# A two-layer GraphSAGE block with residual and layer norm: the stages of a node block moved and spaced otherwise, h2 produced turned, half-bank strips, degrees as rows

## The chip, the cores and the metric

The kernel runs on one core of one Trainium2 chip. The time is that of the device, in microseconds (us), as the median of several runs. Each profile is one execution of its own, recorded by the hardware profiler; its time and its span, from the first to the last instruction, are given beside the median.

The core's engines are named as in the profile: PE is TensorE's matmul, PEld its weight load, DVE VectorE, ACT ScalarE, POOL GpSimd, and SP SyncE, which here only starts DMA transfers.

## The reference, cut to what matters

12,500 nodes with 256 features each, 200,000 directed edges, sorted by their destination. `src` is uniform; `dst` is 12500 times the square of a uniform number, so low node numbers have many edges and high ones few. All is float32.

```python
def _sage_conv(x, src, dst, W_l, b_l, W_r):
    msgs = x[src]
    agg = jax.ops.segment_sum(msgs, dst, num_segments=N_NODES)
    deg = jax.ops.segment_sum(jnp.ones((src.shape[0],), x.dtype), dst, num_segments=N_NODES)
    mean = agg / jnp.maximum(deg, 1.0)[:, None]
    return mean @ W_l + b_l + x @ W_r

h = jax.nn.relu(_sage_conv(x, src, dst, W1_l, b1, W1_r))
h = jax.nn.relu(_sage_conv(h, src, dst, W2_l, b2, W2_r))
out = _layernorm(x + (h @ W3 + b3), axis=-1)        # eps 1e-5, no scale, no shift
```

All six weights and products are 256 by 256. The output has 12,500 rows of 256.

## The kernel before, in words

*Units.* The nodes are cut into NB = 98 blocks of 128 (P). D is 256 and NC = 2 is the number of 128-wide chunks in it. Two tables of layer results stand in device memory: `h_d` (h in float32) and `h3_d` (each float32 number as three bfloat16 parts, which `exact` makes). `x3_d` is the same split of x; the profile calls these two tables `x_d` and `h_d` in places.

*Two ways to sum neighbours.* The sums of the first nodes, which have many edges, are made by dense products: `count` builds a matrix that tells how often each source occurs for each of DN = 256 destinations, and `product` multiplies the split table with it. This covers HG1 = 5 groups of 256 nodes in layer 1 and HG = 8 in layer 2. The other nodes are summed from gathered rows.

- `count`: DVE builds one-hot pieces (`pick`, `low`, `aft`, L738, L741, L746), PE multiplies them (L765, L776, L780), ACT casts the product into `counts` (L782).
- `product`: SP loads `rows` of the table (L693), two blocks of 128 at a time, and PE multiplies them with the counts into `dense_ps` (L707); in layer 2 a second group goes `beside`, its counts streamed back from memory (L697). ACT copies the result into `d_sb` (L716).
- `degrees`: after each product of layer 1, 98 one-column products for each of the group's two blocks of 128 nodes (L797), with the counts as the stationary matrix and a column of ones as the moving one; DVE takes max(deg, 1) and its reciprocal into a column of `rdeg`.
- `Gathers`: 504 rounds over both layers. `gathered` issues four indirect DMAs on GpSimd's queue (L262), and PE multiplies the rows that landed with a selection matrix `one` into four strips of 32 destinations in `part_ps` (L274). After the last round of a group of edges ACT copies the strips into `some` (L284). `summed` multiplies `some` with a second selection `two` (L290, and L296 for the degrees in layer 1) and DVE adds the result to a ring: the degree row `degs` (L300) and the sums `sums` (L304). The ring is addressed by a register, so every reader of the ring waits for the latest adder.

*A block.* Each block of 128 nodes goes through a generator, whose `yield`s cut it into stages. `first_block`, three stages: load x rows, store the ring's degree row to `deg_d` | read it back as a column, transpose the x rows on PE (L902, copied from PSUM by ACT at L904 into `own_t`) | `sage`: two products with W_l (L925) and two with W_r (L930), zeroing of the ring's part by ACT (L933), two DVE steps with the bias and 1/deg (L936, L937), relu on ACT (L939), then the stores of h and its split. `last_block`, five stages: load the h rows | transpose them (L902) | `sage` | transpose h2 (L902, with `own_t` from L904) | product with W3 (L997), residual, layer norm (L999 to L1008), store (L1010). `agg` is `d_sb` for nodes with dense products and the ring for the others.

*What sets the order.* `layer` (L602) writes the order out by hand. Each round has three places (`part` 0, 1, 2). A place runs, in this order: in part 2, `summed` for the strips that the round before ended; then `pieces`, which moves one block on by one stage and begins another if fewer than MOST = 2 are under way; then `fill`, which takes dense and counting work from a generator until a budget of estimated costs (`COST_DENSE`, `COST_DEGREES` and others, `D_1`, `D_2`) is spent. A stage of a block comes no sooner than APART = 2 places after its last one:

```python
for part in range(3):
    if part == 2 and before:
        gathers.summed(*before, done)
        ...
    pieces()
    fill(spent + (due - spent) / (3 - part))
```

PE and GpSimd execute in the written order. The order on DVE, ACT and SP is the scheduler's, by its own estimates. PSUM is allocated by pools: `mixed_pool` with two banks for the sums and the transposed rows (and, in layer 1, the blocks' products), `part_pool` with one bank for the strips, `dense_pool`, `block_pool`, `beside_pool`, and `count_pool` with two buffers in layer 1 and one in layer 2.

*Tails.* A layer ends when its queue of blocks is empty. `left` keeps the dense work clear of the last 8 rounds of layer 1 and the last 14 of layer 2. A second path, `by_sorting`, is taken for other distributions of edges; it does not run here, and the diff does not touch it.

## Time and profile before

| | |
|---|---|
| runs | 3265.1, 3281.22 and 3290.72 us; median 3281.22 |
| profiled execution | 3281.46 us; span 3279.7 us; mean granted TensorE clock 0.888 |
| busy in the span | PE 2574.5 us, POOL 1967.7, PEld 1733.1, DVE 1566.5, ACT 1151.6 |
| PE, dense products with rows (L707) | busy 981.6 and 570.3 us; idle before them 58.9 and 24.2 |
| PE, counts (L776, L765) | idle before them 145.0 and 77.4 us |
| PE, first products of blocks (L925) | six groups; idle before them 69.7, 85.0, 1.5, 8.6, 5.8 and, for L930, 0.1 us |
| PE, transposes (L902) of x, h2, h | idle before them 6.8, 51.4 and 6.4 us |
| PE, degrees (L797) | busy 40.2 us, idle before them 25.1 |
| DMA | 612.56 MB, mean 187 GB/s |

The span less PE's busy time leaves 705 us in which PE does nothing. A line of a group gives the line number, the engine, the operation, its output and inputs by the program's names, the shape, the number of instructions, then after the first bar the busy time and the mean ns of one, and after the second the idle time of the engine just ahead of these instructions and what ended most of it. In the view of waits a line gives the engine, the output and line that waited, the instruction that ended the wait, and then the sum in us, the number of waits and the longest. In a timeline the columns are the start and the length in us, the engine, the line and the instruction, and in brackets a wait ahead of it with what ended it.

### The profile page before, as it was taken

To read this page: it belongs to the slowest core of one execution; us is meant where nothing else is said; L and a number is where in the kernel's file an instruction comes from. 1 tells how busy PE (TensorE), PEld (TensorE's weight loads), DVE (VectorE), ACT (ScalarE), POOL (GpSimd) and SP (SyncE) were. 2 spreads that over 40 slices of the span, in tenths; PEclk is the share of its full clock that TensorE was granted. 3 is DMA by queue.
4 is the path that set the end of the run, shared out by engine and by line. 5 is a ranking of instruction groups with operands and counts; after the bars stand their busy time and mean duration, and the time that the engine had idled before them with its cause. 6 is when DMAs were issued, how large, how long until landed. Compare 5 with 4: busy or idle time off the path is not lost.

```text
span 3279.7 us, 56146 instructions
## 1 busy us (share of the span) xinstructions
PE 2574.5 (79%) x18946; PEld 1733.1 (53%) x18946; DVE 1566.5 (48%) x5560; ACT 1151.6 (35%) x2331; POOL 1967.7 (60%) x2026
## 2 busy tenths in 40 slices
PE   4565668878878878889865887878889888888876
PEld 2122335545546656656643555556556666666654
DVE  6778675544445555555552122334345444343334
ACT  0423664444444444455441001223233333221122
POOL 6665666666665656666664666565666666556652
PEclk9766679979979989989987899989989999999998
DMA  5565668658658758647644566565556656566642
GB/s 123 164 185 171 179 205 274 209 159 262 209 156 289 225 174 266 221 144 238 222 142 122 181 183 184 176 181 166 177 167 192 184 170 183 164 200 198 204 139 84
DMA packets 375242, 612.56 MB, mean 187 GB/s; under 512 B 72111, under 2 KB 253989, under 8 KB 374949
## 3 DMA queue, kind: packets, MB, share of 16 engines
q1 hardware_dynamic: 273235, 343.33, 34.0%
q0 software_dynamic: 96768, 264.37, 26.7%
q8 instruction: 155, 2.54, 0.3%
q10 hardware_dynamic: 4946, 1.19, 0.2%
q14 instruction: 138, 1.13, 0.1%
HBM read 518.75 MB, written 89.92 MB: 186 GB/s over the span
## 4 chain that ended last, share of the span: by engine, by line
PE 59%; issue 8%; another core or an unknown queue 7%; DVE 5%; ACT 3%; DMA 3%; POOL 0%; ACTq 0%; DVEq 0%; SPq 0%; POOLq 0%
PE dense_ps L707 16%; PE part_ps L274 7%; PE count_ps L776 7%; PE beside_ps L707 6%; PE block_ps L925 6%; PE block_ps L930 5%; PE sum_ps L290 4%; PE block_ps L997 3%; PE block_ps L902 3%; DMA rows<-x_d 2%; ACT counts L782 2%; PE count_ps L780 1%; PE sum_ps L296 1%; PE dense_ps L797 1%
## 5 line engine op out<-in xcount | busy, mean ns | idle before, releaser
L262 POOL DMA_INDIRECT got<-in_x_dram,src_t x1076 | 1067.8, 992 | 649.6 <-issue 258.2
L262 POOL DMA_INDIRECT got<-h_d,src_t x940 | 897.7, 955 | 617.1 <-issue 230.8
L707 PE MATMUL dense_ps<-counts,rows 128*128 128x256 bf16 x5292 | 981.6, 282 | 58.9 <-issue 31.5
L707 PEld LDWEIGHTS <-rows 128*128 128x128 bf16 x7644 | 745.2, 101 | 327.6 <-issue 165.6
L782 ACT CAST counts<-count_ps 128x882 f32 (+3 forms) x688 | 611.3, 888 | 533.1 <-PE count_ps L776 135.6
L707 PE MATMUL beside_ps<-spare,rows 128*128 128x256 bf16 x2352 | 570.3, 282 | 24.2 <-issue 23.2
L776 PE MATMUL count_ps<-pick,low 128*128 128x490 bf16 (+2 forms) x1188 | 378.7, 371 | 145.0 <-ACT counts L782 64.3
L274 PE MATMUL part_ps<-got,one 128*32 128x257 f32 (+1 forms) x4032 | 385.4, 434 | 53.2 <-issue 21.7
L738 DVE TENSOR_SCALAR pick<-steps,key_t 128x686 bf16<-128x686 f16 (+3 forms) x816 | 332.6, 410 | 117.6 <-remote 32.1
L218 DVE TENSOR_TENSOR one<-lo_t,lane_b 128x128 f32<-128x128 bf16 x504 | 144.1, 286 | 470.7 <-remote 150.1
L284 ACT COPY some<-part_ps 128x257 f32<-128x257 f32 (+1 forms) x355 | 132.8, 374 | 643.4 <-remote 293.7
L741 DVE TENSOR_SCALAR low<-lanes,low_t 128x130 bf16<-128x130 f16 x816 | 221.0, 272 | 212.4 <-remote 72.5
L304 DVE TENSOR_TENSOR sums<-sums,sum_ps 128x256 f32 x355 | 145.6, 410 | 250.2 <-remote 110.6
L290 PE MATMUL sum_ps<-two,some 128*128 128x128 f32 x1420 | 241.1, 296 | 13.1 <-issue 8.3
L290 PEld LDWEIGHTS sum_ps<-two,some 128*128 128x128 f32 x1420 | 211.2, 207 | 32.2 <-issue 19.3
L776 PEld LDWEIGHTS <-low 128*128 128x128 bf16 x1188 | 121.1, 103 | 181.9 <-issue 62.7
L936 DVE TENSOR_TENSOR own<-block_ps,biases 128x256 f32<-128x256 f32 x196 | 82.4, 420 | 220.3 <-PE block_ps L930 106.5
L274 PEld LDWEIGHTS part_ps<-got,one 128*32 128x32 f32 x4032 | 89.1, 113 | 184.1 <-issue 161.1
L925 PE MATMUL block_ps<-w1l_sb,sums 128*128 128x256 f32 x352 | 123.5, 483 | 69.7 <-issue 31.5
L933 ACT COPY sums<-zero 128x256 f32<-128x256 f32 x170 | 68.7, 404 | 306.0 <-PE block_ps L930 142.6
L904 ACT COPY own_t<-block_ps 128x256 f32<-128x256 f32 x294 | 109.3, 375 | 183.4 <-remote 65.4
L746 DVE TENSOR_SCALAR aft<-steps,after_t 128x98 bf16<-128x98 f16 x689 | 173.6, 252 | 0.0
(184 smaller groups left out, 2678.7 us busy)
## 6 DMA issues: line engine op xcount, KB each, us to landing
rows<-x_d SPq DMA_DIRECT2D x245, 384.0 KB
rows<-h_d SPq DMA_DIRECT2D x196, 384.0 KB
count_d<-counts SPq DMA_DIRECT2D x28, 896.0 KB
spare<-count_d SPq DMA_DIRECT2D x196, 128.0 KB
x_sb<-in_x_dram SPq DMA_DIRECT2D x194, 128.0 KB
x_d<-split SPq DMA_DIRECT2D x98, 192.0 KB
h_d<-split SPq DMA_DIRECT2D x98, 192.0 KB
got<-in_x_dram,src_t POOLq DMA_INDIRECT x1076
```

What stands on the lines that cost most here:

```text
L262: rows = nc.gpsimd.indirect_dma_start(out=g[:, j, :D], out_offset=None, in_=self.table, in_offset=bass.IndirectOffsetOnAxis(ap=src_t[:, e: ...
L274: strip = nc.tensor.matmul(part_ps[j * W:(j + 1) * W, :width], lhsT=one[:, j], rhs=g[:, j, :width], start=r == 0, stop=r == n - 1)
L290: nc.tensor.matmul(sum_ps[:, c], lhsT=some[:, c * P:(c + 1) * P], rhs=two, start=True, stop=True)
L304: nc.vector.tensor_add(own, own, sum_ps[:, :NC])
L707: nc.tensor.matmul(t[:, c], lhsT=rows[:, b % 2, k, c * P:(c + 1) * P], rhs=d, start=False, stop=b == NB - 1 and k == 2 and c == NC - 1)
L738: nc.vector.tensor_scalar(r[:, :w * NB], steps[:, :w * NB], key_t[g][:, t - lo_g:t - lo_g + 1], None, op0=OP.is_equal)
L741: nc.vector.tensor_scalar(low.rearrange("p (a b) -> p a b", a=5), lanes_5[:, :, :LW // 5], low_t[:, t:t + 1], None, op0=OP.is_equal)
L746: nc.vector.tensor_scalar(aft.rearrange("p (a b) -> p a b", a=7), steps_7[:, :, :NB // 7], after_t[g][:, t - after_from[g]:t - after_from[ ...
L776: nc.tensor.matmul(c[:, a * NB:b * NB], lhsT=s, rhs=r[:, a * NB:b * NB], start=True, stop=alone)
L782: nc.scalar.copy(to[:, :, bass.ds(off_act.at(t), w)], c.rearrange("p (d s) -> p s d", s=NB))
L925: product = nc.tensor.matmul(ps[:, 0], lhsT=agg[:, c], rhs=wl[:, c], start=c == 0, stop=c == NC - 1)
L930: product = nc.tensor.matmul(ps[:, 1], lhsT=own_t[:, c], rhs=wr[:, c], start=c == 0, stop=c == NC - 1)
```

## The change

Four things are changed; the numbers of the lines in this section are those of the kernel before.

1. *Order and distance.* `pieces` stands ahead of `summed` in a place. Each stage yields the number of places to the next one: SOON = 2 from a block's loads to its transposes, APART = 4 after that.
2. *h2 turned.* In `last_block` the weights become the stationary matrices and the turned sums and rows the moving ones, so that the products come out with the features of h2 on the partitions. There are eight products of 128 columns in the place of four of 256. 1/deg is now needed along the free axis: the degree row is read from `deg_d` broadcast to 128 partitions (`r_sb`). The bias of layer 2 is a column for each partition (`b2_t`), added by ACT with the relu, in two halves. The transposes of h2 and their copy are gone, and with them one stage of five. `sage` is dissolved into the two blocks.
3. *Strips.* `part_ps` is one bank allocated once; layer 2's groups of rounds use its halves in turn.
4. *Degrees as rows.* In `degrees` the ones are the stationary matrix and the counts the moving one: 490 products with one output row of 256 columns in the place of 980 with one output column. Max and reciprocal are taken on the row, which is stored to `deg_d`. For blocks of the ring, max and reciprocal are taken on the ring's row before it is stored. Every block now reads its degrees back from `deg_d`, and `rdeg` is gone. `D_1`, layer 1's estimated cost of a dense group, falls accordingly.

```diff
+    part_bank = part_pool.tile([P, 2 * D], F32, name="part_ps")
@@ gathered
-            if r == 0:
-                self.part_ps = part_pool.tile([P, D + 1], F32, name="part_ps")
-            part_ps, width = self.part_ps, self.width
+            width = self.width
+            half = gr % 2 * D if self.second else 0
+            part_ps = part_bank[:, half:half + width]
@@ layer
-    MOST, APART = 2, 2
+    MOST, SOON, APART = 2, 2, 4
...
-                next(p)
-                queue.append([b, p, n_pieces - 1, turn + APART])
+                queue.append([b, p, n_pieces - 1, turn + next(p)])
...
-                next(q[1])
-                q[2:] = q[2] - 1, turn + APART
+                q[2:] = q[2] - 1, turn + next(q[1])
...
             for part in range(3):
+                pieces()
                 if part == 2 and before:
                     gathers.summed(*before, done)
                     ...
-                pieces()
                 fill(spent + (due - spent) / (3 - part))
@@ degrees
-        for j in range(DN // P):
-            for b in range(NB):
-                nc.tensor.matmul(ps[:, 0, j:j + 1], lhsT=c_sb[:, b, j * P:(j + 1) * P], rhs=ones_b,
-                                 start=b == 0, stop=b == NB - 1)
-                if b % 14 == 13:
-                    yield COST_DEGREES
-        deg = work.tile([P, DN // P], F32, name="d_deg", bufs=1)
-        nc.vector.tensor_scalar(deg, ps[:, 0, :DN // P], 1.0, None, op0=OP.max)
-        nc.vector.reciprocal(rdeg[:, n0:n0 + DN // P], deg)
+        for b in range(NB):
+            nc.tensor.matmul(ps[0:1, 0], lhsT=ones_b, rhs=c_sb[:, b, :DN], start=b == 0, stop=b == NB - 1)
+            if b % 14 == 13:
+                yield COST_DEGREES
+        deg = work.tile([1, DN], F32, name="d_deg", tag="own")
+        nc.vector.tensor_scalar(deg, ps[0:1, 0], 1.0, None, op0=OP.max)
+        nc.vector.reciprocal(deg, deg)
+        nc.sync.dma_start(deg_d[n0:n0 + DN // P].rearrange("b p -> (b p)")[None, :], deg)
-    D_1 = NB * COST_DENSE + DN // P * (NB // 14) * COST_DEGREES
+    D_1 = NB * COST_DENSE + NB // 14 * COST_DEGREES
@@ first_block
             agg, deg_row = ring(b)
+            nc.vector.tensor_scalar(deg_row, deg_row, 1.0, None, op0=OP.max)
+            nc.vector.reciprocal(deg_row, deg_row)
             nc.sync.dma_start(deg_d[b:b + 1], deg_row)
-        yield True
+        yield SOON
-        if of_ring:
-            deg = work.tile([P, 1], F32, name="deg")
-            with nc.allow_non_contiguous_dma(reason="a row becomes a column"):
-                nc.sync.dma_start(deg, deg_d[b, :, None])
+        deg = work.tile([P, 1], F32, name="deg")
+        with nc.allow_non_contiguous_dma(reason="a row becomes a column"):
+            nc.sync.dma_start(deg, deg_d[b, :, None])
         x_t, copied = transposed(x_sb, turned(), "own_t")
-        yield True
-        if of_ring:
-            nc.vector.tensor_scalar(deg, deg, 1.0, None, op0=OP.max)
-            nc.vector.reciprocal(rdeg[:, b:b + 1], deg)
-        h, own = sage(x_t, copied, b, agg, of_ring, w1l_sb, w1r_sb, biases[:, 0], "h")
+        yield APART
+        # the products, DVE steps and relu of sage, written out, with deg for rdeg[:, b:b + 1]
+        ...
@@ last_block
-        h2, _ = sage(h_t, copied, b, agg, of_ring, w2l_sb, w2r_sb, biases[:, 1], "h")
+        r_sb = work.tile([P, P], F32, name="r_sb")                # ahead of the transposes
+        nc.sync.dma_start(r_sb, deg_d[b:b + 1].to_broadcast([P, P]))
...
+        ps = block_bank()
+        for side, (t, w) in enumerate(((agg, w2l_sb), (h_t, w2r_sb))):
+            for o in range(NC):
+                for c in range(NC):
+                    product = nc.tensor.matmul(ps[:, side, o * P:(o + 1) * P], lhsT=w[:, c, o * P:(o + 1) * P],
+                                               rhs=t[:, c], start=c == 0, stop=c == NC - 1)
+                    ...
+        if of_ring:
+            zeroed(agg, product)
+        own = work.tile([P, NC, P], F32, name="own")
+        nc.vector.tensor_tensor(own, ps[:, 0].rearrange("p (c l) -> p c l", c=NC),
+                                r_sb.unsqueeze(1).to_broadcast([P, NC, P]), op=OP.mult)
+        nc.vector.tensor_add(own, own, ps[:, 1].rearrange("p (c l) -> p c l", c=NC))
+        h2_t = work.tile([P, NC, P], F32, name="h")
+        for c in range(NC):
+            nc.scalar.activation(h2_t[:, c], own[:, c], AF.Relu, bias=b2_t[:, c:c + 1])
         x_sb = load_rows(x, N, b, "x_sb")
-        yield True
-        h2_t, _ = transposed(h2, turned(), "own_t")
-        nc.vector.tensor_add(x_sb, x_sb, biases[:, 2])
-        yield True
+        yield APART
+        nc.vector.tensor_add(x_sb, x_sb, biases[:, 1])
         y = block_bank()
...
-    layer(Gathers(h_d, True), last_block, 5, staged(stages_2), cost_of(stages_2), 14)
+    layer(Gathers(h_d, True), last_block, 4, staged(stages_2), cost_of(stages_2), 14)
```

More of the change, by code (lines that the diff above doesn't have):

```diff
@@ L283, in gathered @@
             some = chosen_pool.tile([P, D + 1], F32, name="some", bufs=2)
-            nc.scalar.copy(some[:, :width], part_ps[:, :width])
+            nc.scalar.copy(some[:, :width], part_ps)
             return gr, some, two
@@ L919, in overlap, with zeroed @@
                 nc.scalar.copy(degs[:, RN:], zeros[0:1, 0])
[L921 to L940 removed]
+    def zeroed(agg, product):
+        cleared = nc.scalar.copy(agg, zeros)
+        tc.add_manual_dep(cleared.ins, product.ins.name, LANDED, reason="it signals for all")
     def block_bank(turned=False):
@@ L982, in last_block @@
         of_ring = agg is None
-        yield True
+        yield SOON
         if of_ring:
```

55 lines of the change are left out of this document (27 added, 28 removed).

## The prediction

> **What bounds the kernel now.** I read the page's busy times first, then the tensor engine's waits, then its groups with shapes kept apart, and last the timeline for the pace of each kind of product.
>
> ```profile
> PE 2574.5 (79%) x18946; PEld 1733.1 (53%) x18946; DVE 1566.5 (48%) x5560; ACT 1151.6 (35%) x2331; POOL 1967.7 (60%) x2026
> ```
>
> ```profile
> PE count_ps L776 <- ACT counts L782: 64.3, 52, 9.9
> PE block_ps L925 <- issue: 46.7, 26, 4.5
> ...
> PE block_ps L925 <- DVE sums L304: 36.4, 24, 6.4
> ...
> PE block_ps L902 <- ACT h L939: 34.6, 29, 3.7
> ...
> PE block_ps L925 <- ACT own_t L904: 29.4, 12, 5.8
> PE dense_ps L707 <- DMA rows<-x_d: 26.3, 19, 5.7
> ```
>
> The tensor engine is busy 2574.5 of 3279.7 us, nothing else comes near. GpSimd is not the limit: four gathers of 1.25 us make 5.0 us a round, rounds come every 6.1 to 6.5 us, and in the view of all waits GpSimd stands 332.7 us waiting for strips (L274). So the 705 us in which PE is idle are the price list. The lines of blocks (L925, L902, L997) hold 247 us of them by the groups, and these are what the change works on.
>
> ```profile
> L902 PE MATMUL block_ps<-ident,h 128*128 128x128 f32 x196 | 42.8, 302 | 51.4 <-ACT h L939 34.6 <-issue 14.4 <-ACT own_t L904 1.2
> L797 PE MATMUL dense_ps<-ones_b,counts 128*128 128x1 bf16 x980 | 40.2, 165 | 25.1 <-issue 18.2 <-ACT d_sb L716 6.4 <-DMA h_d<-split 0.5
> ```
>
> The mean of one record (302 ns) is its latency; the pace is the distance of two starts:
>
> ```profile
> 661.46 0.49 PE L797 MATMUL dense_ps<-ones_b,counts 128*128 128x1 bf16 x14 [2.03 <-ACT d_sb L716]
> 661.81 0.37 PE L776 MATMUL count_ps<-pick,low 128*128 128x490 bf16 x1
> ```
>
> ```profile
> 3061.19 0.27 PE L707 MATMUL beside_ps<-spare,rows 128*128 128x256 bf16 x1
> 3061.30 0.61 PE L290 MATMUL sum_ps<-two,some 128*128 128x128 f32 x4
> 3061.75 0.38 PE L902 MATMUL block_ps<-ident,h 128*128 128x128 f32 x2
> 3061.96 0.27 PE L707 MATMUL dense_ps<-counts,rows 128*128 128x256 bf16 x1
> ```
>
> So 14 one-column products take 0.35 us (25 ns each), 256 bfloat16 columns 0.11, four records of 128 float32 columns 0.45 (an instruction in float32 leaves two records), and the two transposes of a block 0.21.
>
> The last view shows a first product that waits for the sums:
>
> ```profile
> 1302.27 0.22 PE L296 MATMUL sum_ps<-two,some 128*1 128x128 bf16 x1
> ...
> 1302.94 0.64 PE L274 MATMUL part_ps<-got,one 128*32 128x257 f32 x8
> 1305.05 0.27 DVE L300 TENSOR_TENSOR spare<-spare,sum_ps 1x128 f32 x1 [1.73 <-PE part_ps L274]
> 1305.26 0.40 DVE L304 TENSOR_TENSOR sums<-sums,sum_ps 128x256 f32 x1
> 1305.81 0.45 PE L925 MATMUL block_ps<-w1l_sb,sums 128*128 128x256 f32 x1 [2.22 <-issue]
> ```
>
> L925 reads the ring, so it waits for the latest L304, here until 3.5 us after the sum's products; "issue" hides that cause. To price this, I took for each of the 196 blocks the PE work that stands in program order between the last sum and its first product (columns at the pace above), beside the idle time ahead of that L925 in the timeline (layer 2 without its tail after 3100 us):
>
> | work since the last sum, us | layer 1: blocks, mean idle | layer 2 |
> |---|---|---|
> | under 0.8 | 11, 1.58 | 7, 1.32 |
> | 0.8 to 1.1 | 18, 1.98 | 1, 6.38 |
> | 1.1 to 1.5 | 8, 1.35 | 11, 1.01 |
> | 1.5 to 2 | 11, 0.38 | 0 |
> | 2 to 3 | 22, 0.08 | 22, 0.15 |
> | 3 to 5 | 17, 0.08 | 26, 1.47 |
> | over 5 | 11, 0 | 13, 0.23 |
>
> A product within 1.5 us of a sum waits; later ones do not, except 3 to 5 us in layer 2, where nine wait for the copy of the turned rows (ACT own_t, up to 5.8 us) at two places' distance.
>
> **The change, part by part**, against the profiled execution: 3281.5 us, of which 3279.7 are its span; it stands at the median, 3281.2.
>
> *The transposes of h2 go.* 98 pairs of 0.21 us are 21 us, 23 at the granted clock of 0.888; with them the 51.4 us of idle. The wait for ACT's relu moves to the product with W3 four places later, over 8 us of other work where 2 to 3 us stood. I take 47 of the 51 as gone (some "issue" will show elsewhere): -70, between -75 and -50 (half of the idle returns). ACT loses a copy (0.375) and a relu of 256 columns (0.416) and gets two of 128, between the 0.295 of L1005 and 0.416: nothing on PE's path while ACT is 35% busy.
>
> *h2 from stationary weights.* Eight products of 128 columns for four of 256: sixteen records at the pace of L290 take 1.80 us; L925 and L930 take 0.94 and 0.87. So 0, up to +15. The page "TensorE: Matmul & The Clock Gate" of the Trainium skill (Back-to-back issue gap) says that the spacing of matmuls with a fresh weight load each is set by both, about 81 ns at 128 columns where the columns alone take 56; L290, a fresh load for each product, shows none of that here. By that ratio of the Trainium skill the sixteen records would take some 2.6 us, an estimate, and the 98 blocks +78 us.
>
> *Degree rows.* 980 one-column products (24.5 us at full clock, 27.6 at 0.888, and 25.1 idle: 52.7) become 490 of one output row and 256 columns. No row has that form. Below: the pace of L707, 0.109, so 53 us at full clock. Above: L296, also one output row, takes 0.15 for 128 columns (664.67 to 664.82), so 0.20 for 256, 112 us at 0.888. L707 is nearer, since a new weight load also stands ahead of each and the instructions follow each other: 60 us, +8, between 0 and +59.
>
> *Four places apart, ahead of the sums.* The order of instructions in the built kernel shows that a block now starts at part 0, is turned at part 2 and has its first product at part 0 again, right behind the strips, whatever the round: in layer 1 the seven rows of the table hold 17, 29, 24, 13, 6, 5 and 4 blocks, in layer 2 (all 98) 11, 7, 43, 10, 2, 15 and 10. With one sum in two rounds the old distance dodged the sum and the new one meets it. Layer 1: 7.8 and 4.3 us of the idle in the first row were single waits for the degree column and a zeroing, which four places remove; without them its mean is 0.59. Then 105.6 us stand against 59.1, +46, and with the two single waits gone +34. Layer 2: the wait for own_t goes (0.15 in the row of 3 to 5; I put 1.2 and 0.4 for the rows with one and no block), 75 us for 98 blocks, 64 for the 84 ahead of the tail, against 71: -7. Bounds by the waits themselves: 0 to +75 and -40 to +30.
>
> *What moves with it.* The fill is paced by costs, and D_1 shrinks from 91 to 80: rows of x_d are asked for earlier (37 loads with under 6 us of work ahead of their use, 71 before), counts follow ACT less closely (118 with under 1.5 us, 154 before). These two waits hold 90 us; I take -20, between -45 and 0. Strips in halves: -3 (L274 waits for "some" 5 us in all).
>
> *Small work.* 98 row loads, 10 columns and 5 rows join SP's queue, 113 of up to 0.42 us, 47 us of a queue that is free most of the time; 64 KB each are 6 MB of 613. Four places cover their landing. In layer 1 max and reciprocal on a row of 128 precede the store, up to 0.28 each by L300 (0.15 on columns), ahead of SP's deg_d store and of the next L300, which may not overwrite the row until it is stored: +5, between 0 and +15.
>
> *Tails.* Behind the last dense product stand 14 blocks and 14 rounds in both. Now 6 blocks, not 4, remain behind the last strips, one chain: products 1.8, two DVE steps 0.9, relu, W3 0.9, DVE 0.4 and handovers, 5.5 us each, 33 for 25. The rounds before hold less and come nearer to 5 us than their 6.6: 0, between -10 and +15.
>
> *Clock.* At 1567.6 a wait of 2.17 us is followed by granted clocks of 0.50 and 0.65 in two windows of 2 us, 1.6 us lost; waits under 2 us leave no such trace. About ten such waits come in layer 1, and about as many at L902 and own_t go: -5, between -20 and +20. The Trainium skill's page "TensorE: Matmul & The Clock Gate" (The HAM clock gate) puts the fall behind an idle window of 3.4 us; here 2.2 us was enough, and by the Trainium skill this term would be nearer 0.
>
> Sum: -70 + 0 + 8 + 34 - 7 - 20 - 3 + 5 + 0 - 5 = -58, so 3223 us.
>
> **Rivals.** *The waits only move* (3287): if what is late is the tensor engine's own signal (at 2207.7 ACT, SP and DVE all wake together after PE had recorded the transpose at 2199.0), the idle of L902 and own_t returns at the next dependence: +47 and +17. Against it: most of L902's waits are 0.8 to 2.5 us behind a relu that plainly ended just before. Degrees at 0.20 us (+52, 3275) have the same answer.
>
> *The sums decide* (3371, slower): 122 first products outside the tail stand within 1.5 us of a sum. If each waits 2.0 us, as the row 0.8 to 1.1 does, that is +81 in layer 1 and +40 in layer 2 instead of +34 and -7 (+87 beyond the forecast), and if one in two passes 2 us, the clock adds 61. For it: the table, and that L304 starts a median 2.2 us behind the sum in 1000 to 1600 us. Against: layer 2 has no L300 and its row shows 1.0. It decides from a mean of 1.65 us per first product, where the gain is gone.
>
> *Weight loads show* (3380): if the products of 128 columns wait for their loads (207 ns by PEld's mean at L290, sixteen of them 3.3 us for 1.8), 98 blocks pay 147 us, some 157 at the clock. L290's pace denies it. The issue-gap rule of the Trainium skill's page "TensorE: Matmul & The Clock Gate", cited above, speaks for it.
>
> **How the numbers follow.** Forecast 0.50; the waits move or the degrees cost double 0.22; the sums 0.25; the loads 0.03. About 1% (33 us) is what a measurement here can tell from no change: the forecast is faster, the second group within, the last two slower. The bounds of the terms, taken as independent, give about 65 us down; upward I let the range reach through the second group to the lower end of the sums: 3155 to 3320.
>
> **What would show it.** No L902 on h and 0.1 us or less idle at the W3 product outside the tail; sixteen records in 1.8 us; degree products 0.11 apart; layer 1's first products idle 100 to 110 us, layer 2's 60 to 70, with DVE sums or "issue" as releaser; own_t under 5 us in all. Wrong if the first products idle over 250 us, or if the idle freed at L902 stands again at L776 or L707.

## The result, and the profile after

The changed kernel takes 3306.2 us (median of 7 runs, 3292.5 to 3314.5), the kernel before 3279.4 us on the same chip: a ratio of 1.0074, 95% interval 1.0052 to 1.0096. It is slower by three quarters of a per cent. The forecast was 58 us faster; the profiled execution is 28.6 us slower (3310.0, span 3307.9).

The page of the changed kernel, busy times:

```profile
PE 2573.9 (78%) x19044; PEld 1768.1 (53%) x19044; DVE 1630.8 (49%) x5560; ACT 1153.8 (35%) x2331; POOL 1981.5 (60%) x2026
```

The tensor engine works as long as before (2574.5), so the 28 us are idle time. Next, the view of stretches, first of the kernel before, then of the changed one, cut at the end of layer 1's last degree product, at the start of layer 2 and at its last dense product. The columns are the length and the busy time of PE, PEld, DVE, ACT and POOL with their instructions, the granted clock, the DMA share and GB/s.

```profile
0.00:1691.30 1691.30, 1288.65 (x9489) 808.57 (x9490) 988.37 (x3697) 762.94 (x1467) 1050.84 (x1066) 0.86 0.66 202
1691.30:1745.70 54.40, 36.80 (x218) 26.15 (x215) 27.50 (x96) 20.25 (x58) 19.17 (x20) 0.84 0.41 122
1745.70:3155.30 1409.60, 1171.20 (x8839) 844.67 (x8838) 498.96 (x1609) 338.07 (x720) 855.87 (x896) 0.92 0.60 180
3155.30:3279.70 124.40, 77.91 (x410) 53.72 (x407) 51.68 (x159) 30.29 (x86) 41.79 (x44) 0.87 0.31 90
```

```profile
0.00:1717.50 1717.50, 1293.24 (x9005) 811.13 (x9005) 1060.53 (x3702) 770.40 (x1467) 1065.05 (x1067) 0.86 0.65 198
1717.50:1775.10 57.60, 40.79 (x210) 27.96 (x207) 34.41 (x98) 21.82 (x60) 19.84 (x20) 0.79 0.41 121
1775.10:3179.90 1404.80, 1160.74 (x9344) 868.67 (x9343) 484.54 (x1604) 333.02 (x721) 856.03 (x898) 0.92 0.62 184
3179.90:3307.90 128.00, 79.09 (x493) 60.34 (x490) 51.33 (x157) 28.51 (x86) 40.58 (x43) 0.82 0.33 93
```

Layer 1 loses 26 us, its tail 3, layer 2's tail 4, and layer 2 itself, which was to win some 80, wins 5. What fills it is seen in the waits of the tensor engine over layer 2 (the third stretch):

```profile
PE block_ps L990 <- ACT some L284: 49.7, 9, 6.6
PE block_ps L990 <- DVE sums L304: 48.9, 17, 7.2
```

and in two groups over the whole span that answer to the ones shown of before:

```profile
L1008 PE MATMUL block_ps<-w_sb,h 128*128 128x256 f32 x392 | 111.3, 405 | 37.0 <-ACT h L1002 28.7 <-issue 7.1 <-DVE own L997 0.6
...
L797 PE MATMUL dense_ps<-counts,ones_b 128*1 128x256 bf16 x490 | 59.9, 273 | 4.8 <-issue 4.8
```

The 51 us of idle ahead of the transposes of h2 are gone with the transposes, and ahead of the last tail the W3 product waits only 6 of its 37 us. But layer 2's first products (L990) now wait 129 us where L925 waited 71. The waits are long: nine of them, put down to the strips' copy, hold 49.7 us together.

One of those waits, in the timeline of the changed kernel (start, length, engine, line, instruction; in brackets the idle time ahead and what ended it):

```profile
1959.63 0.61 PE L290 MATMUL sum_ps<-two,some 128*128 128x128 f32 x4
1959.70 0.95 POOL L262 DMA_INDIRECT got<-h_d,src_t  x1 [0.30 <-issue]
...
1961.72 0.38 PE L274 MATMUL part_ps<-got,one 128*32 128x256 f32 x1 [0.26 <-issue]
1962.21 0.94 POOL L262 DMA_INDIRECT got<-h_d,src_t  x1 [0.30 <-issue]
1963.46 0.94 POOL L262 DMA_INDIRECT got<-h_d,src_t  x1 [0.30 <-issue]
1964.71 0.95 POOL L262 DMA_INDIRECT got<-h_d,src_t  x1 [0.30 <-issue]
1967.46 0.42 DVE L304 TENSOR_TENSOR sums<-sums,sum_ps 128x256 f32 x1 [8.28 <-remote]
1967.60 0.32 SPq L694 DMA_DIRECT2D rows<-h_d  x1
1967.66 0.37 ACT L284 COPY some<-part_ps 128x256 f32<-128x256 f32 x1 [10.67 <-remote]
...
1967.84 0.95 POOL L262 DMA_INDIRECT got<-h_d,src_t  x1 [2.18 <-remote]
...
1968.03 1.19 PE L990 MATMUL block_ps<-sums,w2l_sb 128*128 128x128 f32 x4 [5.94 <-ACT some L284]
```

The sum's products end at 1960.2 and the strips at 1962.1. DVE, ACT and SP start nothing between 1959.7 and 1967.4, and GpSimd, which is busy with gathers until 1965.7, then pauses for 2.2 us. After that all four start within 0.4 us, though by the program each waits for another product. So no engine was slow: the tensor engine's signals came over 5 us late.

The trace also records updates of semaphores, the signals by which the engines wait for each other, and this gives a measure: for each product that signals, the time from its recorded end to the engine's next recorded update. In the changed kernel its mean is 1.10 us (a quarter over 1.68, 5% over 4.05, 1% over 6.2), in the kernel before 1.09. The measure has two weak sides. The end of a product is modelled by the profile, and the trace holds fewer updates than there are instructions that signal (2485 for 2929 of the tensor engine, 2268 for 4037 of DVE, 1316 for 2300 of ACT), so that a single delay may be read too long. The starts of the engines that wait say the same without it. Where ACT stands idle, its copy of the strips (L284) starts 1.54 us in the median behind their last product; in the run without gathers below it is 0.07. Between DVE and ACT there is no such delay: the square root of the layer norm (ACT L1016) starts 0.04 us behind the DVE instruction that it needs, and DVE's L1018 0.03 us behind the square root. After the last gather of the span the tensor engine's signals, too, come within 0.04 us.

### The profile page after: what moved, and what is told of

It is laid out like the page before. It is cut to its first block, busy times and chain, and to the rows that moved or that the text cites. A ratio compares the mean times of both kernels' runs of the same rounds, so it can differ in the third digit from the quotient of the medians.

```text
span 3307.9 us, 56483 instructions
## 1 busy us (share of the span) xinstructions
PE 2573.9 (78%) x19044; PEld 1768.1 (53%) x19044; DVE 1630.8 (49%) x5560; ACT 1153.8 (35%) x2331; POOL 1981.5 (60%) x2026
## 3 DMA queue, kind: packets, MB, share of 16 engines
q14 instruction: 141, 1.16, 0.1%
## 4 chain that ended last, share of the span: by engine, by line
PE 65%; another core or an unknown queue 10%; DVE 8%; issue 8%; ACT 3%; DMA 2%; DVEq 1%; POOL 0%; SPq 0%; ACTq 0%
PE dense_ps L708 16%; PE part_ps L274 8%; PE block_ps L990 7%; PE count_ps L777 7%; PE beside_ps L708 7%; PE sum_ps L290 5%; PE block_ps L954 4%; PE block_ps L959 3%; PE block_ps L1008 3%; PE dense_ps L797 2%; PE block_ps L902 2%; DVE pick L739 1%; ACT counts L783 1%; PE count_ps L781 1%
## 5 line engine op out<-in xcount | busy, mean ns | idle before, releaser
L262 POOL DMA_INDIRECT got<-in_x_dram,src_t x1076 | 1082.7, 1006 | 662.4 <-issue 263.8
L708 PE MATMUL dense_ps<-counts,rows 128*128 128x256 bf16 x5292 | 971.3, 280 | 41.3 <-issue 27.6
L777 PE MATMUL count_ps<-pick,low 128*128 128x490 bf16 (+2 forms) x1188 | 363.4, 359 | 153.1 <-ACT counts L783 57.2
L274 PE MATMUL part_ps<-got,one 128*32 128x257 f32 (+1 forms) x4032 | 396.1, 428 | 68.9 <-issue 29.7
L284 ACT COPY some<-part_ps 128x257 f32<-128x257 f32 (+1 forms) x355 | 132.5, 373 | 686.7 <-remote 274.4
L990 PE MATMUL block_ps<-sums,w2l_sb 128*128 128x128 f32 x656 | 114.2, 327 | 127.0 <-ACT some L284 49.7
L990 PEld LDWEIGHTS block_ps<-sums,w2l_sb 128*128 128x128 f32 x656 | 97.1, 227 | 163.1 <-issue 81.7
```

Of the source, the lines that this page charges most:

```text
L262: rows = nc.gpsimd.indirect_dma_start(out=g[:, j, :D], out_offset=None, in_=self.table, in_offset=bass.IndirectOffsetOnAxis(ap=src_t[:, e: ...
L274: strip = nc.tensor.matmul(part_ps[j * W:(j + 1) * W], lhsT=one[:, j], rhs=g[:, j, :width], start=r == 0, stop=r == n - 1)
L708: nc.tensor.matmul(t[:, c], lhsT=rows[:, b % 2, k, c * P:(c + 1) * P], rhs=d, start=False, stop=b == NB - 1 and k == 2 and c == NC - 1)
L777: nc.tensor.matmul(c[:, a * NB:b * NB], lhsT=s, rhs=r[:, a * NB:b * NB], start=True, stop=alone)
L990: product = nc.tensor.matmul(ps[:, side, o * P:(o + 1) * P], lhsT=w[:, c, o * P:(o + 1) * P], rhs=t[:, c], start=c == 0, stop=c == NC - 1)
```

## The experiments

Two theories stood at the start. S: first products lose their time because they meet the sum of the ring. M: the tensor engine's own signals are late, so a wait that is taken away comes back at the next dependence. The runs fell on chips of two kinds, which was learned on the way: the kernel before takes 3242 to 3284 us on those of the first result and the first eight runs, and 2743 to 2747 us on three others. Ratios are therefore always to the kernel before on the same chip, and stage lengths are compared only within a kind.

### Three places in the place of four

```diff
-        yield APART      # after the transposes, both blocks
+        yield 3
```

> The changed kernel with one number altered: from a block's transposes to its first products three places instead of four. In the written order nearly all first products then stand over 2 us of tensor work behind the latest sum (87 of 96 in layer 1, 80 of 98 in layer 2; 12 and 27 in the changed kernel). If the first products lose their time because they meet the sum (theory S), their idle falls from 229 us ahead of the tails to about 60, and the time by some 150 us, to 3130 to 3190. If the tensor engine's own late signals are the cause and a wait only moves to the next dependence (theory M), the idle goes elsewhere and the time falls by less than 50 us, to 3255 or more.

Measured: 3284.7 us, before 3284.3; ratio 1.0006 (0.9986 to 1.0026). The first products behaved as S says: 32 us idle in layer 1 (98 in the changed kernel) and 32 in layer 2 (129). The time fell by 0.7%, some 22 us, as M says. Groups of the tensor engine over layer 2 (1758.5 to 3148.6 us of this run), then the same lines of the changed kernel:

```profile
L708 PE MATMUL dense_ps<-counts,rows 128*128 128x256 bf16 x2351 | 585.9, 287 | 44.2 <-issue 42.1 <-DMA out_dram<-z 0.8 <-DMA got<-h_d,src_t 0.4
L708 PE MATMUL beside_ps<-spare,rows 128*128 128x256 bf16 x2350 | 584.8, 286 | 37.5 <-issue 36.6 <-DVE two L224 0.2
L274 PE MATMUL part_ps<-got,one 128*32 128x256 f32 x1768 | 178.8, 404 | 51.7 <-issue 26.6 <-DMA got<-h_d,src_t 14.9 <-ACT some L284 7.8
...
L990 PE MATMUL block_ps<-sums,w2l_sb 128*128 128x128 f32 x576 | 83.2, 288 | 24.4 <-issue 19.2 <-DVE z L1010 3.4 <-ACT some L284 0.9
```

```profile
L708 PE MATMUL dense_ps<-counts,rows 128*128 128x256 bf16 x2351 | 567.2, 281 | 18.6 <-issue 17.9
L708 PE MATMUL beside_ps<-spare,rows 128*128 128x256 bf16 x2351 | 565.5, 280 | 21.0 <-issue 20.4 <-DMA got<-h_d,src_t 0.2
L274 PE MATMUL part_ps<-got,one 128*32 128x256 f32 x1768 | 164.8, 407 | 33.6 <-issue 13.8 <-DMA got<-h_d,src_t 12.7 <-ACT some L284 6.3
...
L990 PE MATMUL block_ps<-sums,w2l_sb 128*128 128x128 f32 x576 | 100.7, 328 | 122.7 <-ACT some L284 49.7 <-DVE sums L304 48.9 <-issue 15.3
```

The 98 us that L990 gives back stand again, 60 of them, at the dense products and the strips; the tensor engine is also busy 21 us more in this stretch.

### Order and distances of before

```diff
-    MOST, SOON, APART = 2, 2, 4       # and pieces() ahead of summed
+    MOST, SOON, APART = 2, 2, 2       # and pieces() behind summed
```

> The changed kernel with the order and the distances of the kernel before: two places throughout, the stages behind a place's sums. Turned h2, half-bank strips and degree rows stay. S: layer 1 is back at the kernel before within 15 us; layer 2's first products still stand near a sum (50 of 97 within 1.5 us), and the product with W3 comes two places behind the relu, where the kernel before waited 51 us at the transposes; the transposes' 21 us of work are saved: 3255 to 3285. M: the same sum of waits as in the kernel before, so 3255 to 3265. What tells more is the idle of the W3 product: 30 us or more if the relu is late at two places, under 10 if not.

Measured: 3418.5 us, ratio 1.0421 (1.0397 to 1.0445), outside both expectations. Layer 2 takes 1516.9 us (1409.6 before, 1404.8 changed), and the W3 product there waits:

```profile
L1008 PE MATMUL block_ps<-w_sb,h 128*128 128x256 f32 x336 | 105.9, 444 | 102.0 <-ACT h L1002 67.6 <-issue 26.4 <-DVE own L999 5.4
```

The transposes of h2 and the W3 product of before waited 55 us together in that stretch, and here their one successor waits 102. So turned h2 does not pay at two places on this chip; the four places are what makes it bearable. The waits did not keep their sum either, as M would have it in its plain form.

### First products that need no sum

```diff
-            agg, _ = ring(b)
+            agg, mine = w3_sb[:, :, :P], ring(b)[0]     # last_block; mine is what is cleared
```

> The changed kernel, in which layer 2's first products of blocks with gathered rows read a constant (a part of W3) in the place of the ring: the neighbour sums are left out of h2, while all sums are still made and cleared. The products then depend on no sum. S: the 129 us of idle at layer 2's first products ahead of the tail nearly vanish (under 20), and the time falls by 80 to 115 us, to 3190 to 3225. M: the wait reappears at the next product that needs something from ScalarE or VectorE (counts, sums), and the time falls by less than 40 us.

Measured: 3280.6 us, ratio 0.9992 (0.9969 to 1.0015), 0.8% or some 27 us under the changed kernel. L990's two sides still wait 47 us in layer 2, now mostly put down to "issue", and strips 47.5 for 33.6, rows 52 for 40. M's bound (less than 40 us) holds; S asked for 80 to 115.

### No gathers

```diff
+                if i >= NGOT:          # rounds after the first four of a layer
+                    continue
                 rows = nc.gpsimd.indirect_dma_start(
```

> The changed kernel with gathers in the first four rounds of each layer only; the strips multiply rows that stay in the buffers. All other instructions stay. In the changed kernel the tensor engine's signals reach the other engines up to 6 us after the recorded end of its products, but promptly after the last gather. M (the gathers delay the signals): waits of first products fall to about 1 us each with none over 2.5, and the idle of the tensor engine falls by 300 us or more. S alone (the delay is the engines' queues): first products still wait 2 us where they stand behind a sum, about 150 us in all; the time falls only by what GpSimd held up.

Measured: 2566.5 us (one run), 740 us less. The page:

```profile
span 2564.2 us, 53008 instructions
...
PE 2321.0 (91%) x19044; PEld 1658.1 (65%) x19044; DVE 1615.5 (63%) x5560; ACT 1156.6 (45%) x2331; POOL 35.7 (1%) x42
```

The signals' mean delay is 0.025 us. The tensor engine's idle time is 243 us for 734, and the same 19044 products are busy 253 us less, at a granted clock of 0.954 for 0.885. First products wait 6.6 us in layer 1 and 8.2 in layer 2. On this chip the signals are late with gathers and prompt without them; the engines' own queues, which hold the same work as before, do not make them late. Not all of the 740 us are late signals, though: where signals are prompt in any case, the gathers still cost some 200 us (2761.4 us with them, 2564.7 without, on two such chips below).

### Degree rows and halves alone

The kernel of the run with the old order, its `last_block` put back to the five stages of before, and in it

```diff
-        r_sb = work.tile([P, P], F32, name="r_sb")
-        nc.sync.dma_start(r_sb, deg_d[b:b + 1].to_broadcast([P, P]))
+        deg = work.tile([P, 1], F32, name="deg")
+        nc.sync.dma_start(deg, deg_d[b, :, None])
```

> The kernel before with degree rows and half-bank strips only: old order, old distances, h2 transposed as before in five stages (its 1/deg read back as a column). Turned h2 is out, so the run before this one with the old order (3418 us), less this one, is what turned h2 costs at two places' distance. M (a waiting dependence costs what the signal's delay makes it, wherever it stands): degree rows add 98 x 5 products of 0.11 us where 980 of 0.025 stood, 27 us for 25 plus the idle they had, and a store and a read for each block; within 1% of the kernel before, 3260 to 3310, and turned h2 at two places costs the rest, 110 us or more. Rival (degree rows and their fill costs disturb layer 1): layer 1 ends 25 us or more later than in the kernel before, and the time is 3300 or more.

Measured: 3272.0 us, before 3242.5 on this chip; ratio 1.0093 (1.0061 to 1.0125). Within M's 1%. The kernel before was not profiled on this chip; beside its first profile, layer 1's first products wait 87 us for 56, with the old order, and layer 2's 44 for 71. So most of layer 1's longer wait in the changed kernel (98) does not need the new order. Turned h2 at two places is the rest of the 4.2% (across two chips): about 3.3%, some 107 us, near what M put on it.

### An eighth of the bytes

```diff
-                    out=g[:, j, :D], out_offset=None, in_=self.table,
+                    out=g[:, j, :D if i < NGOT else 32], out_offset=None,
+                    in_=self.table if i < NGOT else self.table.rearrange("n (k f) -> (n k) f", f=32),
```

> The changed kernel with all 2016 gathers, but after the first four rounds each row that is gathered is 32 numbers long in the place of 256: the same instructions on GpSimd, an eighth of the bytes; the sums are of other rows then. If the bytes that land delay the tensor engine's signals, the mean delay of a signal behind its product's recorded end falls from 1.10 us towards the 0.03 us of the run without gathers and the time towards 2600 to 2800 us, held up by GpSimd alone (504 rounds of 5.0 us are 2520). If GpSimd's instruction itself does it (1.25 us each, unchanged), the delay stays near 1 us and the time above 3200.

Measured: 3253.5 us on the chip of the run above (one run), mean delay 1.09 us. The bytes that land are not it; what is left is GpSimd's gather instruction and what it sets off besides the data.

### Two buffers for gathered rows

```diff
-    NGOT = 4
+    NGOT = 2
```

> The changed kernel with two buffers for gathered rows instead of four, so that GpSimd runs two rounds ahead and pauses more often. If the tensor engine's signals pass in the pauses between gathers, long delays become rarer (95% of them now under 4.1 us) and first products wait less, but each round now depends on a signal two rounds back: 3300 to 3400. If the delay does not hang on the pauses, the signals stay as late and the time is 3400 or more.

Measured: 3274.7 us, ratio 1.0088 (1.0058 to 1.0119), below both expectations and the changed kernel's own loss within the intervals. The delay is 1.05 us in the mean, 5% over 3.74 (4.05 with four buffers): hardly rarer. First products wait less (73 and 74 us), strips more (106 and 98): another wait that only moved.

GpSimd hardly paused more: for 1756 us of this span one gather starts within 1.35 us of the last, with four buffers for 1803. That signals pass in the pauses is shown by the changed kernel's own trace. Of the products that end while the next gather starts within 1.35 us of the last, 58% signal over 0.5 us late, 1.44 us in the mean. Of those that end in a longer pause, 1.5 us or more behind the start of the last gather, it is 10%, and 0.22 us in the mean. In pauses of over 4 us, from 0.5 us behind the last gather on, the median delay is 0.014 us.

### Own rows first

```diff
-        for side, (t, w) in enumerate(((agg, w2l_sb), (h_t, w2r_sb))):
+        for side, (t, w) in reversed(tuple(enumerate(((agg, w2l_sb), (h_t, w2r_sb))))):   # on the three places
```

> The run with three places from the transposes to the first products (3284.7 us), with layer 2's products of a block's own rows put ahead of those of the ring: 0.9 us of work that needs no sum covers part of each wait. S: the 34 us of idle at layer 2's first products fall to under 15 and the time by 15 to 25 us, 3260 to 3270. M: what falls there returns elsewhere, 3275 to 3290.

Measured: 3251.0 us, ratio 1.0026 (1.0006 to 1.0047). Three places alone stood at 1.0006, so nothing is gained: M. What waits is still the first of the two, now the own rows' product (35 us, as much as before), though it needs no sum; the ring's product behind it waits 3 us. Over 1740 to 3120 us of this run:

```profile
L990 PE MATMUL block_ps<-own_t,w2r_sb 128*128 128x128 f32 x672 | 96.7, 288 | 34.9 <-issue 19.0 <-DVE z L1010 9.1 <-ACT some L284 2.4
L990 PE MATMUL block_ps<-sums,w2l_sb 128*128 128x128 f32 x576 | 79.0, 280 | 3.0 <-issue 2.9
```

### On chips with prompt signals

The next three kernels, and the kernel before beside them, fell on a chip where the kernel before takes 2743.1 us with all its gathers.

```diff
+                if j == 3 and i >= NGOT:     # three of four strips gather
+                    continue
```

> The changed kernel in which, after the first four rounds, each round gathers three of its four strips' rows; the fourth strip multiplies rows left in its buffer. All else stays. A: GpSimd's gathers and the pauses in which the tensor engine's signals pass set the pace of a round (now 5.0 us and some 1.3 us): a round falls by the 1.25 us of one gather, 504 of them by up to 630 us, and the time to 2700 to 2900. B: each gather adds its own share of delay to a kernel that the tensor engine sets: a quarter of the 740 us that all gathers cost, 3080 to 3160.

Measured: 2609.6 us. The expectation was for late signals, and here they are prompt (0.017 us), so the run decides between neither. It lies near the changed kernel without any gathers on this chip:

> The changed kernel without gathers after the first four rounds of each layer once more, on the chip of the kernel before without them: 2530 to 2570 us, 20 to 60 us below it if turned h2 and the longer distances are worth what the forecast put on them, within 10 us if not.

> The kernel before with gathers in the first four rounds of each layer only (the sums of gathered rows are then of stale rows). With it the changed kernel without gathers is run again on the same chip. If the forecast's working was sound for waits that are priced at prompt signals, the changed kernel gains here what it did not gain with gathers: the transposes' 21 us of work and their waits, so this run is 20 to 60 us slower than the changed kernel without gathers. If the change is worth nothing in itself, both are within 10 us.

Measured: the changed kernel without gathers 2564.7 us (on the chip with late signals 2566.5), the kernel before without them 2543.8. Without gathers the two kinds of chips are alike. And the change loses there too, 21 us, against what both alternatives said. By stages: layer 1 1357.0 us for 1326.9, where the degree products are busy 53.0 us for 25.8; layer 2 1069.7 for 1080.8. So without gathers 27 of layer 1's 30 us are the degree products' own work.

```diff
-    COST_DENSE, COST_DEGREES, COST_SPLIT = 0.7, 1.6, 0.8
+    COST_DENSE, COST_DEGREES, COST_SPLIT = 0.7, 0.8, 0.8      # kernel before
```

> The kernel before with one estimated cost changed: a degree step is put at 0.8 in the place of 1.6, which gives layer 1's dense groups the cost that they have in the changed kernel (80 for 91) and only moves where the fill stands in the rounds; not one instruction is added or removed. If the interleaving alone makes the loss of degree rows (+0.9% with the old order), this run is 0.5 to 1.2% slower than the kernel before. If the rows themselves make it (490 products of 256 columns, max and reciprocal ahead of the store), it is within 0.3%.

Measured: 2715.5 us, ratio 0.9886 (0.9861 to 0.9911). It is faster, not slower. A shift of the fill's pace, without one instruction more or less, moves this kernel by 1.1%. It is the only version with all its gathers that is faster than the kernel before; it was tried only on a chip with prompt signals, and the changed kernel was not run with its gathers on that one.

The changed kernel, the kernel before, and two versions on another chip of this kind:

> The changed kernel itself on the chip of this call. If signals are prompt here (kernel before near 2743 us): what it loses without gathers, 24 us, holds, so 0.5 to 1.3% slower; if late signals were its only loss, it is faster by 20 us or more. If they are late here: 0.4 to 1.2% slower, as in the first result.

> The kernel before, for its stages on this chip. With prompt signals: first products and transposes of h2 wait under 30 us in all, where 247 us stood at the blocks' lines in the profile that the prediction read; with late ones, as there.

Measured: the change 2761.4 us against 2746.9, ratio 1.0052 (1.0031 to 1.0073). The kernel before, profiled at 2740.4: its first products, transposes of h2 and W3 products, which waited 233 us in the first profile, wait 40 here (36 without the W3 products, where under 30 was expected). Layer 2 over its stretch, first the kernel before, then the changed one:

```profile
L274 PE MATMUL part_ps<-got,one 128*32 128x256 f32 x1768 | 141.7, 391 | 72.4 <-DMA got<-h_d,src_t 71.0 <-ACT counts L782 1.1
...
L902 PE MATMUL block_ps<-ident,h 128*128 128x128 f32 x168 | 33.6, 282 | 1.0 <-ACT some L284 0.7 <-ACT h L939 0.3
```

```profile
L274 PE MATMUL part_ps<-got,one 128*32 128x256 f32 x1768 | 141.7, 391 | 83.5 <-DMA got<-h_d,src_t 80.6 <-ACT own_t L904 2.7
```

Here GpSimd's gathers are what the tensor engine waits for. GpSimd issues 898 and 900 gathers in these stretches, which at 1.25 us are 1123 and 1125 us of their 1151.1 and 1144.1. Of the 23 us of transposes that the change takes out, 11 come back as waits for gathered rows. The waits of GpSimd tell the same from the other side, in the first profile of before and in this one:

```profile
POOL got L262 <- PE part_ps L274: 332.7, 135, 10.6
```

```profile
POOL got L262 <- PE part_ps L274: 99.9, 79, 8.0
```

The changed kernel's profile on this chip is 550 us shorter than its first one, on a chip with late signals. The tensor engine is idle 395 us for 734 and busy 2363 for 2574, at a granted clock of 0.950 for 0.885. So late signals go with idle time and also with slower work.

```diff
-        for b in range(NB):                       # degrees() of the changed kernel
-            nc.tensor.matmul(ps[0:1, 0], lhsT=ones_b, rhs=c_sb[:, b, :DN], ...)
+        for j in range(DN // P):                  # as before; 1/deg stored to deg_d as columns
+            for b in range(NB):
+                nc.tensor.matmul(ps[:, 0, j:j + 1], lhsT=c_sb[:, b, j * P:(j + 1) * P], rhs=ones_b, ...)
```

> The changed kernel with dense groups' degrees as columns again: 980 products of one column at 25 ns, 1/deg stored as columns. All else is the change (ring blocks' rows, order, turned h2, halves). With prompt signals 27 us of degree work come off layer 1, and what is left of the change gains the 11 us of layer 2: 0.2 to 0.8% faster than the kernel before. If the degree rows are not what costs, it stays as slow as the changed kernel. With late signals: the two within 0.7% of each other, either way.

> Degree columns and three places from the transposes to the first products. With prompt signals the first products wait little in any case (15 us without gathers), so within 0.4% of the version with columns alone; with late signals 0.3 to 1.0% below it, as three places were below four.

Measured: 2786.7 us (ratio 1.0143, 1.0114 to 1.0171) and 2826.9 (1.0273, 1.0233 to 1.0314). Both are slower than the change, against both expectations. The degree products are busy 27 us again in layer 1 instead of 55, and yet layer 1 takes 1482.6 and 1515.7 us for 1457.9; its strips wait 68 us for 42 in the first, its first products 29 for 8.5 in the second.

Two more, on a third chip of this kind (before 2745.9 us): columns at the change's pace, and the old order and distances in layer 1 alone.

```diff
-    COST_DENSE, COST_DEGREES, COST_SPLIT = 0.7, 1.6, 0.8      # the degree columns of above
+    COST_DENSE, COST_DEGREES, COST_SPLIT = 0.7, 0.8, 0.8
```

> The changed kernel with dense groups' degrees as columns again (980 products at 25 ns), but at the changed kernel's own pace: a degree step is put at 0.8, a dense group at 80. If pace and products add up (pace -28 us, rows +27 us, both on chips with prompt signals), this run is 20 to 30 us below the changed kernel: 0.3 to 0.6% faster than the kernel before on such a chip. If they do not add, and each shift of the written order makes its own time, it is anywhere from 1% faster to 1.5% slower. On a chip with late signals: within 0.7% of the changed kernel's +0.7%.

```diff
-        yield APART         # first_block of the changed kernel
+        yield 2             # and pieces() behind summed in layer 1
```

> The changed kernel with layer 1 in the order and the distances of the kernel before (two places, stages behind the sums); layer 2 as changed. The run with degree columns at the old pace lost 41 us in layer 1 against the kernel before on the same chip, which leaves the order and the distances there as the cause. If they are, layer 1 ends 20 to 40 us earlier than in the changed kernel and the time is 0.3 to 1% below the kernel before on a chip with prompt signals. If not, it stays within 0.3% of the changed kernel. On a chip with late signals: layer 1's first products wait about as long (87 us with the old order, 98 with the new), so within 0.5% of the changed kernel.

Measured: 2765.6 us (ratio 1.0078, 1.0052 to 1.0104) and 2768.8 (1.0097, 1.0065 to 1.0130). Neither returns the loss, and the second's median lies above both of its expectations: layer 1 takes 1468.4 and 1466.8 us. The pace is worth some 18 us here (1.43% to 0.78%, on two chips), but the degree products' 29 us of work come back as waits of strips (67 us for 42). What makes layer 1 slower on such chips is not settled: none of the parts that were taken back wins it back, and 1.1% lies in the interleaving alone. The half-bank strips, the ring's degree rows and turned h2 were not taken back on such a chip.

## Why the prediction was wrong

*What bounds the kernel* failed first. The working took the idle time of the tensor engine as a price list whose items can be struck one by one, and GpSimd as "not the limit". The run without gathers shows 740 us that belong to the gathers: some 540 of them go with late signals (3306.2 us against 2761.4 on a chip with prompt ones), the other 200 remain with prompt ones. On such a chip the items are one debt with many addresses: three places took 163 us off the first products ahead of the tails, and 22 off the time. On the other kind of chip, gathers set layer 2's end outright.

*The transposes of h2* (-70): on their lines this came true. 45.5 us of idle and 29.7 of work left layer 2's stretch, and the W3 product waits 0.07 us per block outside the tail. The run with two places shows that it needs the four.

*Layer 2's first products* (-7) are the term that failed by its size. Forecast were 64 us ahead of the tail, measured 129. Of the 87 us between the forecast and the profiled execution it holds 65. The row "1.1 to 1.5" was priced at 1.01 us from 11 blocks; its 38 blocks ahead of the tail now wait 2.15 in the mean, eleven of them 5.6 to 7.2 us. The trace of before had these delays: ahead of the tail six of layer 2's first products wait over 5 us in it, four of them for own_t, and at 2207.7 a signal comes 8 us late. The working gave them to the copy, and struck them out because four places would hide a copy.

*Layer 1's first products* (+34): forecast 100 to 110 us of idle with the two single waits in or out, measured 98 ahead of layer 1's tail and 101 with it. Right in number, but the reason was half wrong: the degree rows with the old order already make 87.

*h2 from stationary weights* (0): the sixteen records take 1.89 us in the median, the eight of before 1.82 and 1.80 us. By an estimate from the Trainium skill's page "TensorE: Matmul & The Clock Gate" (Back-to-back issue gap) it would be some 2.6; the trace does not bear that out for these products.

*Degree rows* (+8): the records stand 0.109 us apart, as taken. Busy time rose by 23 us (54 for 31) and idle fell by 20, so +3. With prompt signals there is no idle to win, and the same step costs 29.

*Counts and rows* (-20): rows -21 as forecast, counts +7. *Halves* (-3): ahead of the tails, strips waited 12 us longer and sums 7, which no term had. *Tails* (0): +3 and +4, with 31 us at the last W3 products, and 27 less at first products and transposes. *Clock* (-5): a granted clock of 0.885 for 0.888. The reading that waits under 2 us leave no trace in the clock does not hold: after the first 300 us the trace of before has 91 periods at half the clock, and 42 of them have no wait of 2 us in the 6.8 us ahead.

*The rivals.* "The waits only move" named the mechanism, down to the signal at 2207.7, and was argued away by most of L902's waits ending right behind a relu. Its price, 3287, added only two items. "The sums decide" named the place; its threshold of 1.65 us per first product was not reached (238 us over 196 products are 1.2), and taking the place away won almost nothing. Its price has a slip: +81 and +40 for +34 and -7 are 94 us beyond the forecast, not 87. "Weight loads show" is refuted by the pace.

## What to carry to other kernels

Before an idle gap is priced, look at who else wakes at its end. If several engines that wait for different products of one engine start together, microseconds after those products ended, the gap may belong to the signal's path, as it did here, and moving the dependence then only moves the gap. Where two engines hold each other by buffers, test the price list with one run that removes a whole item before adding items up, and look at more than one chip before calling a share of a per cent a property of the kernel.

## What the runs showed of the hardware that was not expected

GpSimd's gather instructions can hold back the tensor engine's signals: 1.10 us in the mean and over 6 us at the worst per cent, with full rows as with an eighth of the bytes (1.09), against 0.025 us without gathers. Within one trace they are late while gathers follow each other (1.44 us in the mean) and prompt in long pauses between them (0.014 in the median). What passes between DVE and ACT is prompt in the same trace (0.03 to 0.04 us). It hangs on the chip or on something that goes with it: on three chips with all gathers the mean is 0.02 us, and the kernel before takes 2743 to 2747 us in the place of 3242 to 3284. That the lateness goes with the gathers is shown by taking them out; how the signal is held, and why some chips don't show it, is open. After a wait of 5 to 7 us the eight records of a first product take 2.04 us, elsewhere 1.16; behind the wait shown above, the granted clock was 0.50 from 1966 to 1970 us.
